# A fused softplus correction, additions moved to the head of a step, three pieces of woven work held back, and an early table load

## The chip, the cores and the metric

The kernel runs on one core of a Trainium2 chip. The time is the device time in microseconds (us) of one execution of the whole kernel; the median of several executions is what two versions are compared by. The core has TensorE (PE: matmuls and transposes, with its weight loads listed as PEld), VectorE (DVE), ScalarE (ACT), GpSimd (POOL) and SyncE (SP), which here only issues DMA transfers. Each engine works through its own instructions in the order in which the program issues them, and waits at an instruction until what it reads or overwrites is free.

## The reference

The input x is 8 images of 256 channels and 96 x 96 points in fp32. Layer 0 normalizes x in groups and adds an attention over channels that works on two-dimensional Fourier transforms. Layer 1, where the change lies, normalizes again and adds a linear attention:

```python
xf = x.reshape(B, C, N)
q = softplus(einsum('dc,bcn->bnd', Wq, xf) + bq)          # d = 32
k = softplus(einsum('dc,bcn->bdn', Wk, xf) + bk)
v = einsum('ec,bcn->ben', Wv, xf) + bv
attn_map = einsum('bdn,ben->bde', k, v)
k_sum = sum(k, axis=-1) + EPS
norm = 1.0 / einsum('bnd,bd->bn', q, k_sum)
out = einsum('bnd,bde,bn->ben', q, attn_map, norm)
x = x + out
```

## The kernel before

An image's activations stay in one of two large SBUF buffers (the "arenas"); the other arena holds what the image needs beside them. The kernel goes through the images one after the other. For each it runs `images` (the rest of layer 0), `layer1`, and `output` (adds layer 1's result and stores it, while layer 0 of the next image begins). The program is written out in the order in which each engine is to work; there is no scheduler that reorders it.

**Woven work.** While image b is in `images`, `layer1` and `output`, the generator `pair_sums(b + 1)` gathers sums of products for the next image. `weave` resumes it as often as the number that the running stage yields; fractions add up. Call each resumption a product: it issues four matmuls (L343) for one third of a group `u` (u = 0 to 11, then a short one for u = 12). In its first third a group also makes the next group's operands, `pair(u + 1)`: for even u + 1 one addition on GpSimd (L391) and one subtraction on VectorE (L392), for odd ones both on GpSimd. In its second third it turns blocks for the group after that, `turn_blocks(u + 2)`: two 32 x 32-block transposes of 128 x 768 on VectorE (L369), ahead of them for even ones two small copies (L364, L365), and after odd ones a DMA that stores both halves of the turned blocks to DRAM (`xtd`, L372) and the load of further input. "Turn 12", the last, is short (L356, L358), and is stored to `xtm` (L359). It writes into the place that the `xtd` transfer after turn 11 reads.

**layer1.** Group statistics on VectorE (L308) and small matmuls (`gm_b`, `gv_b`, `l1b`) give the scaled weights `wkq`. Then come three parts:

- the *kq stage*: for s = 0 to 5 and c = 0 (k) and 1 (q), eight matmuls fill a PSUM tile of 128 x 384 (L812). VectorE stores max(z + bias, 0) in `kq(c, s)` (L814); ScalarE stores exp(-|z + bias|) in `ex` (Abs L816, Exp L817). PSUM tiles of this tag are five in rotation.
- the *kx loop*: softplus is max(z, 0) + log(1 + e). The function `softplus(c, s)` forms u = 1 + e on VectorE (L834), the rounding error (u - 1) - e (L835), lets ScalarE take log(u) (L836) and subtracts the error from z (L837); `close()` later adds the logarithm (L843). Per step s, TensorE transposes k (L867, copied by ScalarE, L868), then three times a piece of x (eight transposes into two PSUM tiles, L878, copied by L881 on ScalarE or L883 on VectorE), and sums k times x in `kx` (L850). The q parts of softplus are worked off in the second half of the loop.
- the *end*: `kx` is copied (`kxs`, L897) and transposed (`kxT`), k's sum gives the denominators (`den`, L917), VectorE forms their reciprocals (`rec`, L921), and at the start of `output` matmuls spread them (L946).

The generator's yields in `layer1` are 2 and 1 in the statistics, 2 ahead of the kx loop, and three times 1 at the end.

Of the kernel before, what the change touches and what calls it, by code (L numbers as in the profile page):

```python
# [73 lines left out]
def two_layer_kernel(ctx: ExitStack, tc: tile.TileContext, x, w1t, b1, w2t, b2, w3, b3, wot, temp,  # L74
                     wqt, bq, wkt, bk, wvt, bv, gavg, gmat, tmat, out):
    nc = tc.nc
    B, C, H, W = x.shape
# [3 lines left out]
    CH = 384  # L81
# [3 lines left out]
    NS = NC // NB  # L85
# [9 lines left out]
    one = ctx.enter_context(tc.tile_pool(name="one", bufs=1))  # L95
    two = ctx.enter_context(tc.tile_pool(name="two", bufs=2))
# [22 lines left out]
    def ps_tile(name):  # L119
        return psum.tile([P, 512], F32, tag="ps", name=name)  # L120
# [57 lines left out]
    for j in range(4):  # L178
        s = slice(32 * j, 32 * j + 32)
# [20 lines left out]
    epsb = const.tile([P, 1], F32, name="epsb")  # L200
# [131 lines left out]
    s0 = {}  # L332
    R2 = 0.5 ** 0.5

    def pair_sums(b):

        acc = [acc_tile(f"acc{c}_{b}") for c in range(2)]
        CB = C + 2
# [37 lines left out]
        def pair(u):  # L376

            eo = ring_tile(f"eo_{b}_{u}").rearrange("p (q c n) -> p q c n", q=NQ, c=2)
            nq, np_ = (NQ, P) if u < NG else (1, W)
            ft, gt = (t[0:np_, 0:nq, u % 2] for t in turned(b))  # L380
            e, o = (eo[0:np_, 0:nq, c, 1:C + 1] for c in range(2))
            nc.gpsimd.memset(eo[0:np_, 0:nq, :, 0:CB:CB - 1], 1.0 if u < NG else R2)  # L382
            if u == 0:
                nc.gpsimd.memset(eo[0:32, 0:nq, :, 0:CB:CB - 1], R2)
            if u in (0, NG):
                w = R2 if u else pw
                nc.vector.tensor_scalar_mul(o, gt, w)
                nc.vector.scalar_tensor_tensor(e, in0=ft, scalar=w, in1=o, op0=ALU.mult, op1=ALU.add)
                nc.vector.scalar_tensor_tensor(o, in0=ft, scalar=w, in1=o, op0=ALU.mult, op1=ALU.subtract)
            else:  # L390
                nc.gpsimd.tensor_add(e, ft, gt)  # L391
# [4 lines left out]
        ahead = pair(0)  # L396
        turn_blocks(1)
        yield
        for u in range(NG + 1):
            eo, nq, np_ = ahead  # L400
            for q in range(nq):
                if q == 0 and u < NG:
                    ahead = pair(u + 1)
                if q == 1 and u + 2 <= NG:
                    turn_blocks(u + 2)
                if (u, q) == (NG - 1, 1):
                    wl = ring_tile(f"wl_{b}")[:, 0:6 * C].rearrange("p (k o) -> p k o", k=KC)
                    for o, v in enumerate((w1t, w2t, w3)):
                        nc.sync.dma_start(out=wl[:, :, o * C:(o + 1) * C], in_=v.rearrange("(k p) o -> p k o", p=P))
                products(eo, q, np_, u == 0 and q == 0, u == NG)  # L410
                yield
# [258 lines left out]
    def images(b):  # L670
# [53 lines left out]
        for i in range(NC):  # L724
            if i % 8 == 0:
                v16 = []
# [33 lines left out]
            if i >= WI:  # L760
                yield 2.5 if i > WI else 1
        for p in pending:
            yield 1
            project(*p)
        st1s[b] = st1

# [2 lines left out]
    def layer1(b):  # L769
# [7 lines left out]
        nc.sync.dma_start(out=wvs, in_=wvt.rearrange("(k p) o -> p k o", p=P))  # L777
        for k in range(KC):
            nc.scalar.activation(wkq[:, k], wkq0[:, k], AF.Copy, scale=rstd[:, k:k + 1])
        pb = ps_tile(f"l1b_{b}")  # L780
        for c in range(2):
            for k in range(KC):
# [9 lines left out]
        def columns_of(s, j):  # L792

            return (s, 2 * NS - 1 - s, 2 * NS + s, NC - 1 - s)[j] * CH
# [3 lines left out]
        def kq(c, s):  # L798


            k, i = ((s // 2, s % 2) if s < 4 else (0, s - 2)) if c == 0 else ((1, s + 2) if s < 4 else (0, s))
            o = LO + NS * CH + i * CH
            return y_of(b)[:, k, o:o + CH]

        for s in range(NS):
            n = slice(s * CH, (s + 1) * CH)
            for c in range(2):
                ps = ps_tile(f"kq_{b}_{s}_{c}")
                for k in range(KC):
                    for j in range(NB):  # L810
                        o = columns_of(s, j)
                        nc.tensor.matmul(ps[32 * j:32 * j + 32, 0:CH], lhsT=wkq[:, k, c],  # L812
                                         rhs=x[:, k, o:o + CH], start=(k == 0), stop=(k == KC - 1))
                nc.vector.tensor_scalar(kq(c, s), ps[:, 0:CH], scalar1=bkqs[:, c:c + 1], scalar2=0.0,  # L814
                                        op0=ALU.add, op1=ALU.max)
                nc.scalar.activation(ex[:, c, n], ps[:, 0:CH], AF.Abs, bias=bkqs[:, c:c + 1])  # L816
                nc.scalar.activation(ex[:, c, n], ex[:, c, n], AF.Exp, scale=-1.0)  # L817
            if s == 1:
                nmb = own[:, 0:C].rearrange("p (k n) -> p k n", k=KC)
                for k in range(KC):  # L820
                    nc.vector.tensor_scalar_mul(nmb[:, k, :], ones, nmean[:, k:k + 1])
                    nc.vector.tensor_scalar_mul(wvs[:, k, :], wvs[:, k, :], rstd[:, k:k + 1])

        zero = own[:, 5 * C:5 * C + 1]
        nc.scalar.activation(zero, ex[:, 1, NS * CH - 1:NS * CH], AF.Copy, scale=0.0)

        late = []

        def softplus(c, s):

            n = slice(s * CH, (s + 1) * CH)
            z, e = kq(c, s), ex[:, c, n]
            u = two.tile([P, CH], F32, tag="v16", name=f"spu_{b}_{c}_{s}")
            nc.vector.tensor_scalar_add(u, e, 1.0)  # L834
            nc.vector.scalar_tensor_tensor(e, in0=u, scalar=1.0, in1=e, op0=ALU.subtract, op1=ALU.subtract)  # L835
            nc.scalar.activation(u, u, AF.Ln, bias=zero)  # L836
            nc.vector.tensor_sub(z, z, e)  # L837
            late.append((z, u))

        def close():  # L840

            for z, u in late:
                nc.vector.tensor_add(z, z, u)  # L843
            late.clear()
# [12 lines left out]
        softplus(0, 0)  # L857
# [4 lines left out]
        close()  # L862
        nc.vector.tensor_add(bvs, bvs, pv[:, 0:C])
        for s in range(NS):
            pk = ps_tile(f"kT_{b}_{s}")
            for i in range(CH // P):
                nc.tensor.transpose(pk[:, i * P:(i + 1) * P], kq(0, s)[:, i * P:(i + 1) * P], ident)  # L867
            nc.scalar.copy(kq(0, s), pk[:, 0:CH])  # L868
            if s + 1 < NS:
                softplus(0, s + 1)  # L870
            for i in range(s * CH // P, (s + 1) * CH // P):
                xt = [slots[2 * (i % 4) + jj] for jj in range(2)]
                for jj in range(2):
                    pt = ps_tile(f"xT_{b}_{i}_{jj}")
                    for j in range(2):
                        o = columns_of(s, 2 * jj + j) + i % (CH // P) * P
                        for k in range(KC):
                            nc.tensor.transpose(pt[:, j * C + k * P:j * C + (k + 1) * P], x[:, k, o:o + P], ident)  # L878
                    src = pt.rearrange("p (j n) -> p j n", j=2)
                    if jj or i % 6 > 1:  # L880
                        nc.scalar.copy(xt[jj][:, :, 0:C], src)  # L881
                    else:
                        nc.vector.tensor_copy(xt[jj][:, :, 0:C], src)  # L883
                close()
                if s >= NS // 2 and i % (CH // P):
                    softplus(1, 2 * s - NS + i % (CH // P) - 1)
                if len(pend) == 3:
                    for p in pend:
                        add_kx(*p)
                    pend = []  # L890
                pend.append((i, xt, kq(0, s)[:, i % (CH // P) * P:(i % (CH // P) + 1) * P]))
        close()
# [195 lines left out]
```

## Time and profile before

| what | value |
|---|---|
| median of 3 runs | 2651.48 us (2646.25 to 2654.46) |
| the profiled execution's own time | 2650.85 us |
| its span | 2649.0 us |
| TensorE busy | 2509.3 us, 95% of the span |
| VectorE busy | 1789.0 us, 68% |
| ScalarE busy | 1155.9 us, 44% |
| GpSimd busy | 865.6 us, 33% |
| one image, from one `images` to the next | 320.9 us (images 1 to 3) |

The span is the time from the first to the last instruction in the profile; the execution's own time has the launch and the end beside it. Busy time is that of instructions that an engine executes; waiting is idle. A line of the timeline gives the start, the duration, the engine, the line of the kernel, what is written and read with its shape, how many instructions were merged, and in brackets how long the engine had been idle and who released it.

### The profile page before, as it was taken

To read this page: it belongs to the slowest core of one execution; us is meant where nothing else is said; L and a number is where in the kernel's file an instruction comes from. 1 tells how busy PE (TensorE), PEld (TensorE's weight loads), DVE (VectorE), ACT (ScalarE), POOL (GpSimd) and SP (SyncE) were. 2 spreads that over 40 slices of the span, in tenths; PEclk is the share of its full clock that TensorE was granted. 3 is DMA by queue.
4 is the path that set the end of the run, shared out by engine and by line. 5 is a ranking of instruction groups with operands and counts; after the bars stand their busy time and mean duration, and the time that the engine had idled before them with its cause. 6 is when DMAs were issued, how large, how long until landed. Compare 5 with 4: busy or idle time off the path is not lost. (4 is left out here: it accounts for less than half of the span.)

```text
span 2649.0 us, 41157 instructions
## 1 busy us (share of the span) xinstructions
PE 2509.3 (95%) x15580; PEld 1730.2 (65%) x15580; DVE 1789.0 (68%) x3449; ACT 1155.9 (44%) x1985; POOL 865.6 (33%) x817
## 2 busy tenths in 40 slices
PE   3799999999999999999999999999999999999987
PEld 3775666757677576766668566685666757667544
DVE  3457866577756777568675686757866678766766
ACT  0035353453634526344353544435354353534554
POOL 2213514136042451324422343223523135141311
PEclk8899999999999999999999999999999999999999
DMA  9872628637195461935629264492636826286003
GB/s 210 238 216 60 166 71 270 205 67 189 40 313 161 106 173 57 315 120 143 153 90 305 80 167 129 159 316 42 166 89 230 245 60 179 58 289 210 1 7 144
DMA packets 282797, 413.27 MB, mean 156 GB/s; under 512 B 40772, under 2 KB 208872, under 8 KB 282600
## 3 DMA queue, kind: packets, MB, share of 16 engines
q1 hardware_dynamic: 274304, 406.16, 53.2%
q10 hardware_dynamic: 8296, 4.49, 0.8%
q8 instruction: 123, 2.02, 0.3%
q14 instruction: 74, 0.61, 0.1%
HBM read 256.72 MB, written 153.86 MB: 155 GB/s over the span
## 5 line engine op out<-in xcount | busy, mean ns | idle before, releaser
L710 PE MATMUL z<-arena,mz 128*128 128x384 f32 (+1 forms) x2304 | 593.4, 491 | 0.0
L718 PE MATMUL po<-e,wo 128*128 128x384 f32 x1536 | 527.6, 487 | 1.7 <-ACT e L755 1.7
L754 POOL TENSOR_TENSOR e<-e 128x768 f32<-128x768 f32 x192 | 348.4, 1815 | 552.7 <-ACT e L753 529.3
L343 PE MATMUL acc<-eo 128*128 128x257 f32 (+2 forms) x2368 | 437.1, 336 | 50.0 <-POOL eo L382 23.0
L343 PEld LDWEIGHTS acc<-eo 128*128 128x128 f32 (+1 forms) x2368 | 383.8, 194 | 143.9 <-issue 42.4
L710 PEld LDWEIGHTS z<-arena,mz 128*128 128x128 f32 (+1 forms) x2304 | 310.5, 164 | 236.0 <-issue 51.9
L718 PEld LDWEIGHTS po<-e,wo 128*128 128x128 f32 x1536 | 290.0, 190 | 204.7 <-ACT e L755 7.2
L749 DVE TENSOR_TENSOR e<-z,xT 128x768 f32<-128x768 f32 x384 | 361.9, 950 | 75.4 <-PE z L710 74.9
L647 PEld LDWEIGHTS y<-tm,arena 96*128 96x128 f32 x3072 | 365.9, 195 | 52.9 <-issue 18.9
L647 PE MATMUL y<-tm,arena 96*128 96x128 f32 x3072 | 385.7, 281 | 15.3 <-DMA arena<-xtd 6.4
L753 ACT ACTIVATE e<-e 128x1536 f32<-128x1536 f32 x192 | 284.5, 1482 | 195.2 <-DVE e L749 193.3
L391 POOL TENSOR_TENSOR eo<-arena 128x768 f32<-128x768 f32 x88 | 184.5, 2096 | 536.3 <-DVE arena L369 473.2
L720 DVE TENSOR_TENSOR arena<-arena,po 128x384 f32<-128x384 f32 x384 | 209.9, 553 | 190.0 <-PE po L718 190.0
L755 ACT ACTIVATE e<-e 128x768 f32<-128x768 f32 x192 | 162.0, 844 | 367.1 <-POOL e L754 363.2
L986 POOL TENSOR_TENSOR arena<-arena,po 128x384 f32<-128x384 f32 x180 | 179.1, 1014 | 224.0 <-ACT po L985 224.0
L369 DVE STREAM_TRANSPOSE arena<-arena 128x768 f32<-128x768 f32 x192 | 175.7, 953 | 32.5 <-DMA xtd<-arena 23.0
L299 DVE BATCH_NORM_STATS2 st<-arena 128x6 f32<-128x384 f32 x384 | 194.4, 548 | 0.0
L654 ACT COPY ys<-y 128x4 f32<-128x4 f32 (+1 forms) x200 | 32.4, 162 | 363.8 <-DVE arena L653 363.7
L878 PE MATMUL xT<-ident,arena 128*128 128x128 f32 x1152 | 148.4, 277 | 10.0 <-ACT xT L881 9.6
L878 PEld LDWEIGHTS xT<-ident,arena 128*128 128x128 f32 x1152 | 127.2, 142 | 32.0 <-issue 13.6
L985 ACT COPY po<-o 128x384 f32<-128x384 f32 x180 | 79.0, 485 | 157.4 <-PE o L977 152.4
L653 DVE COPY arena<-y 128x384 f32<-128x384 f32 (+1 forms) x200 | 109.1, 546 | 40.8 <-PE y L647 38.6
(225 smaller groups left out, 2493.1 us busy)
## 6 DMA issues: line engine op xcount, KB each, us to landing
xtd<-arena SPq DMA_DIRECT2D x48, 1536.0 KB
arena<-xtd SPq DMA_DIRECT2D x192, 384.0 KB
arena<-in_x_dram SPq DMA_DIRECT2D x96, 768.0 KB
out_dram<-arena SPq DMA_DIRECT2D x192, 384.0 KB
arena<-in_x_dram SPq DMA_DIRECT2D x376, 192.0 KB
tm<-rx SPq DMA_DIRECT2D x96, 159.0 KB
wl<-in_w1t_dram SPq DMA_DIRECT2D x8, 256.0 KB
wl<-in_w2t_dram SPq DMA_DIRECT2D x8, 256.0 KB
```

Of the source, the lines that this page charges most:

```text
L299: nc.vector.bn_stats(out=st[:, k, c, :], in_=x_of(b)[:, k, c * CH:(c + 1) * CH])
L343: nc.tensor.matmul(acc[c][:, m * (C + 1):m * (C + 1) + C + 1 - m * P], lhsT=eo[0:np_, q, c, 1 + m * P:1 + (m + 1) * P], rhs=eo[0:np_, q, c ...
L391: nc.gpsimd.tensor_add(e, ft, gt)
L647: nc.tensor.matmul(pu[:, o:o + P], lhsT=xt[:, s, k * P:(k + 1) * P], rhs=tm[:, n:n + P], start=True, stop=True)
L710: nc.tensor.matmul(out[:, 0:CH].rearrange("p (h q) -> p h q", q=PR), lhsT=columns(mz, k, c, j), rhs=yz[:, k, f, :, o:o + PR], start=(k == ...
L718: nc.tensor.matmul(po[:, 0:CH], lhsT=wo[:, k, m * P:(m + 1) * P], rhs=e[:, k, :], start=(k == 0), stop=(k == KC - 1))
L720: nc.vector.tensor_add(x[:, m, n], x[:, m, n], po[:, 0:CH])
L749: nc.vector.tensor_add(e[:, 2 * c:2 * c + 2, :].rearrange("p t (q h) -> p t q h", h=H), pz[:, 0:CH].rearrange("p (h q) -> p q h", h=H).uns ...
L753: nc.scalar.activation(e, e, AF.Square)
L754: nc.gpsimd.tensor_add(e[:, 0:2, :], e[:, 0:2, :], e[:, 2:4, :])
L878: nc.tensor.transpose(pt[:, j * C + k * P:j * C + (k + 1) * P], x[:, k, o:o + P], ident)
L986: nc.gpsimd.tensor_add(x[:, m, r], x[:, m, r], t)
```

## The change

Layer 0's `pair_sums` gets a way to hold three pieces of its work back: turn 10, pair 10 and turn 11. In images with b > 0 they are put into `held` where they were due, and `layer1` of the image before lets them go: turn 10 after step s = 1 of the kq stage, pair 10 in step s = 3 of the kx loop, turn 11 after `kxs`. Turn 12 and pair 11 are not held. The yields change: the last two projections of `images` yield 1.5 each instead of 1, and `layer1` yields 1 more after the weights are scaled. So every product from the 24th on comes earlier in the program.

A first Exp of one column, `warm`, is issued after the weights are scaled. In the kq stage k's rounding error is formed at once (`rest(0, s)`) and enters the eviction, which becomes one instruction max(z + bias, rest); q keeps its eviction. The scaling of `nmb` and `wvs` moves from s = 1 to s = 2. In the kx loop the logarithm is taken in place with a bias of one, `log(c, s)`; the additions of the logarithm, `close(c, s)`, for k stand first in a step; q is worked off one part per step; the order of TensorE's transposes in a step is x, kx of the step before, x, k, x; and VectorE copies two of a step's six x tiles instead of two in every two steps.

```diff
+    held = {}
+    def release(key):
+        held.pop(key, lambda: None)()
     def pair_sums(b):
+        def prepare(key, step):
+            if b and key in (("turn", 10), ("pair", 10), ("turn", 11)):
+                held[key] = step
+            else:
+                step()
...
                 if q == 0 and u < NG:
-                    ahead = pair(u + 1)
+                    prepare(("pair", u + 1), lambda u=u: make(u + 1))
                 if q == 1 and u + 2 <= NG:
-                    turn_blocks(u + 2)
+                    prepare(("turn", u + 2), lambda u=u: turn_blocks(u + 2))
...
         for p in pending:
-            yield 1
+            yield 1.5
             project(*p)
...
             nc.scalar.activation(wkq[:, k], wkq0[:, k], AF.Copy, scale=rstd[:, k:k + 1])
+        warm = one.tile([P, 1], F32, tag="warm", name=f"warm_{b}")
+        nc.scalar.activation(warm, epsb, AF.Exp)
+        yield 1
...
+        def rest(c, s):
+            e = ex[:, c, s * CH:(s + 1) * CH]
+            u = two.tile([P, CH], F32, tag="v16", name=f"spu_{b}_{c}_{s}")
+            nc.vector.tensor_scalar(u, e, scalar1=-1.0, scalar2=-1.0, op0=ALU.mult, op1=ALU.add)
+            nc.vector.scalar_tensor_tensor(u, in0=u, scalar=1.0, in1=e, op0=ALU.add, op1=ALU.add)
+            return u
...
-                nc.vector.tensor_scalar(kq(c, s), ps[:, 0:CH], scalar1=bkqs[:, c:c + 1], scalar2=0.0,
-                                        op0=ALU.add, op1=ALU.max)
+                pss.append(ps[:, 0:CH])
                 nc.scalar.activation(ex[:, c, n], ps[:, 0:CH], AF.Abs, bias=bkqs[:, c:c + 1])
                 nc.scalar.activation(ex[:, c, n], ex[:, c, n], AF.Exp, scale=-1.0)
+            nc.vector.tensor_scalar(kq(1, s), pss[1], scalar1=bkqs[:, 1:2], scalar2=0.0, op0=ALU.add, op1=ALU.max)
+            nc.vector.scalar_tensor_tensor(kq(0, s), in0=pss[0], scalar=bkqs[:, 0:1], in1=rest(0, s), op0=ALU.add, op1=ALU.max)
             if s == 1:
+                release(("turn", 10))
+            if s == 2:
                 nmb = own[:, 0:C].rearrange("p (k n) -> p k n", k=KC)
...
+        def log(c, s):
+            e = ex[:, c, s * CH:(s + 1) * CH]
+            nc.scalar.activation(e, e, AF.Ln, bias=ones[:, 0:1])
+        def close(c, s):
+            nc.vector.tensor_add(kq(c, s), kq(c, s), ex[:, c, s * CH:(s + 1) * CH])
...
+        log(0, 0)
         yield 2
...
         for s in range(NS):
+            close(0, s)
+            last, pend = pend, []
+            turn_x(3 * s)
+            for p in last:
+                add_kx(*p)
+            turn_x(3 * s + 1)
             pk = ps_tile(f"kT_{b}_{s}")
...
             nc.scalar.copy(kq(0, s), pk[:, 0:CH])
+            turn_x(3 * s + 2)
             if s + 1 < NS:
-                softplus(0, s + 1)
...
+                log(0, s + 1)
+            log(1, s)
+            u = rest(1, s)
+            nc.vector.tensor_add(kq(1, s), kq(1, s), u)
+            if s:
+                close(1, s - 1)
+            if s == 3:
+                release(("pair", 10))
+        close(1, NS - 1)
...
         nc.vector.tensor_copy(kxs, kx[:, 0:C + 1])
         yield 1
+        release(("turn", 11))
```

Here `turn_x(i)` is the body of the old loop over pieces: eight transposes of x and two copies, the first copy on VectorE for i % 3 = 0 and 1.

More of the change, by code (lines that the diff above doesn't have):

```diff
@@ L333, in two_layer_kernel, with make @@
     R2 = 0.5 ** 0.5
+    held = {}
+    def release(key):
+        held.pop(key, lambda: None)()
     def pair_sums(b):
+        ready = {}
+        def prepare(key, step):
[3 more added lines that the diff above has]
+                step()
+        def make(u):
+            ready[u] = pair(u)
         acc = [acc_tile(f"acc{c}_{b}") for c in range(2)]
@@ L395, in pair_sums @@
         turn_blocks(0)
-        ahead = pair(0)
+        make(0)
         turn_blocks(1)
@@ L399, in pair_sums @@
         for u in range(NG + 1):
-            eo, nq, np_ = ahead
+            eo, nq, np_ = ready.pop(u)
             for q in range(nq):
                 if q == 0 and u < NG:
-                    ahead = pair(u + 1)
+                    prepare(("pair", u + 1), lambda u=u: make(u + 1))
                 if q == 1 and u + 2 <= NG:
-                    turn_blocks(u + 2)
+                    prepare(("turn", u + 2), lambda u=u: turn_blocks(u + 2))
                 if (u, q) == (NG - 1, 1):
@@ L803, in kq @@
             return y_of(b)[:, k, o:o + CH]
+        def rest(c, s):
[4 more added lines that the diff above has]
+            return u
         for s in range(NS):
             n = slice(s * CH, (s + 1) * CH)
+            pss = []
             for c in range(2):
@@ L822, in layer1 @@
                     nc.vector.tensor_scalar_mul(wvs[:, k, :], wvs[:, k, :], rstd[:, k:k + 1])
[L824 to L844, printed above, removed]
+        def log(c, s):
[3 more added lines that the diff above has]
+            nc.vector.tensor_add(kq(c, s), kq(c, s), ex[:, c, s * CH:(s + 1) * CH])
         kx = acc_tile(f"kx_{b}")
@@ L856, in layer1, with turn_x @@
         pend = []
-        softplus(0, 0)
+        def turn_x(i):
+            s = i // 3
+            xt = [slots[2 * (i % 4) + jj] for jj in range(2)]
+            for jj in range(2):
+                pt = ps_tile(f"xT_{b}_{i}_{jj}")
+                for j in range(2):
+                    o = columns_of(s, 2 * jj + j) + i % 3 * P
+                    for k in range(KC):
+                        nc.tensor.transpose(pt[:, j * C + k * P:j * C + (k + 1) * P], x[:, k, o:o + P], ident)
+                src = pt.rearrange("p (j n) -> p j n", j=2)
+                if jj or i % 3 == 2:
+                    nc.scalar.copy(xt[jj][:, :, 0:C], src)
+                else:
+                    nc.vector.tensor_copy(xt[jj][:, :, 0:C], src)
+            pend.append((i, xt, kq(0, s)[:, i % 3 * P:(i % 3 + 1) * P]))
+        assert CH == 3 * P
+        log(0, 0)
         yield 2
@@ L861, in layer1 @@
             nc.tensor.matmul(pv[:, 0:C], lhsT=nmb[:, k, :], rhs=wvs[:, k, :], start=(k == 0), stop=(k == KC - 1))
-        close()
         nc.vector.tensor_add(bvs, bvs, pv[:, 0:C])
         for s in range(NS):
+            close(0, s)
[4 more added lines that the diff above has]
+            turn_x(3 * s + 1)
             pk = ps_tile(f"kT_{b}_{s}")
-            for i in range(CH // P):
-                nc.tensor.transpose(pk[:, i * P:(i + 1) * P], kq(0, s)[:, i * P:(i + 1) * P], ident)
+            for t in range(3):
+                nc.tensor.transpose(pk[:, t * P:(t + 1) * P], kq(0, s)[:, t * P:(t + 1) * P], ident)
             nc.scalar.copy(kq(0, s), pk[:, 0:CH])
+            turn_x(3 * s + 2)
             if s + 1 < NS:
-                softplus(0, s + 1)
[L871 to L892, printed above, removed]
+                log(0, s + 1)
[7 more added lines that the diff above has]
+        close(1, NS - 1)
         for p in pend:
```

## The prediction

> **What bounds the kernel now.** I read the page first, for the engines' shares.
>
> ```profile
> span 2649.0 us, 41157 instructions
> PE 2509.3 (95%) x15580; PEld 1730.2 (65%) x15580; DVE 1789.0 (68%) x3449; ACT 1155.9 (44%) x1985; POOL 865.6 (33%) x817
> ```
>
> TensorE is the bound, and a change pays only where it removes idle TensorE time or adds some. So I cut one image (b = 2, not the last) into stages with the busy time by window: statistics to the first `kq` matmul; the `kq` matmuls; from there to `kxT`; `kxT` to the first `rec` matmul; the start of the output.
>
> ```profile
> core 0: us, PE busy (x) PEld busy (x) DVE busy (x) ACT busy (x) POOL busy (x), PEclk, DMA share, GB/s
> 986.93:992.17 5.24, 3.90 (x55) 3.30 (x56) 3.42 (x8) 1.05 (x4) 1.95 (x2) 1.00 0.23 93
> 992.17:1007.76 15.59, 15.59 (x212) 6.11 (x201) 7.87 (x16) 12.27 (x22) 1.73 (x3) 1.00 0.34 101
> 1007.76:1046.34 38.58, 35.30 (x339) 26.04 (x335) 31.53 (x62) 27.36 (x54) 2.04 (x2) 1.00 0.01 1
> 1046.34:1052.69 6.35, 6.05 (x43) 4.24 (x42) 5.47 (x7) 0.59 (x2) 3.14 (x2) 1.00 0.38 156
> ```
>
> The third column is TensorE's busy time: 3.3 us idle in 38.58, 1.3 in the first stage, next to none in the `kq` stage. There VectorE is half empty, and the change fills it. The timeline of TensorE names the waits:
>
> ```profile
> 1012.63 0.55 PE L867 MATMUL kT<-ident,arena 128*128 128x128 f32 x3 [1.11 <-DVE arena L843]
> 1016.31 0.66 PE L878 MATMUL xT<-ident,arena 128*128 128x128 f32 x4 [0.94 <-ACT xT L881]
> 1052.69 0.93 PE L946 MATMUL rec<-rec,sel 32*128 32x384 f32 x8 [0.30 <-DVE rec L921]
> ```
>
> Undisturbed, a step of the kx loop takes TensorE 4.54 us (kT at 1021.43, 1025.97 and 1030.51).
>
> **Three waits that matter later.** From the timelines of GpSimd, VectorE, ScalarE and the DMA queue:
>
> ```profile
> 1012.28 1.99 POOL L391 TENSOR_TENSOR eo<-arena 128x768 f32<-128x768 f32 x1 [18.39 <-DVE arena L369]
> 1012.83 1.71 DVE L834 TENSOR_SCALAR spu<-arena 128x384 f32<-128x384 f32 x1
> ...
> 1004.03 0.62 DVE L814 TENSOR_SCALAR arena<-kq,bkqs 128x384 f32<-128x384 f32 x1 [0.67 <-PE kq L812]
> 1004.68 0.58 ACT L816 ACTIVATE arena<-kq,bkqs 128x384 f32<-128x384 f32 x1 [0.15 <-DVE arena L814]
> ...
> 116.78 0.38 SPq L372 DMA_DIRECT2D xtd<-arena  x1
> 122.10 0.77 DVE L358 STREAM_TRANSPOSE arena<-arena 96x256 f32<-96x256 f32 x2 [5.85 <-issue]
> ```
>
> First, an L834 of 0.35 us took 1.71 while GpSimd's L391 ran; and L391 started as soon as the turn was done, not where its pair stands in the program. Second, ScalarE's Abs starts as VectorE's read of the same PSUM tile ends. Third, turn 12 (L358) sat until 5.3 us after the DMA of turn 11 was issued, because it overwrites what that DMA reads.
>
> [...] in the last image, after 3.61 us idle, three kT matmuls took 0.90 against 0.55.
>
> **The change, part by part.** All in an image that is not the last; "product" is one resumption of the woven pair sums, 1.45 us of TensorE.
>
> *Images' tail and statistics.* The 1.5s bring one product more before the last projection, the new yield one more before `l1b`. Turn 9 comes forward, out of the statistics. Its two transposes (1.8 us on VectorE), 7 DMA issues on SP, then fall under 1.45 + 2.6 us of product and projection, where VectorE waits: nothing. The constant bv and wvs loads queue behind those DMAs, but wvs is needed a step later than before: nothing. The wait for `wkq` (0.93) is filled by the new product. The warm exponential and its table load (1.28 us) run where ScalarE idles 2.46 us: nothing on TensorE; before, the load was hidden too. **-0.95.**
>
> *kq stage.* TensorE delivers a group every 1.29 us. VectorE's work per step was 2 x 0.54; it becomes ts 0.54 + rest 0.38 + 0.59 + the fused eviction 0.62 = 2.15 against 2.58. But the order is stiff: the ts waits for Abs of c = 1 (0.65 after the group), so c = 0's PSUM tile comes free 2.8 us after the step's matmuls. With five tiles the group that reuses it would start after 3.6: backlog allowed, 0.75. Count from the first `kq` matmul. Step 1's eviction ends at 8.1; turn 10, let go here, runs to 10.3 (0.2 + 0.2 + 2 x 0.9). Step 2: ts to 10.8, then rest meets GpSimd's L391 for pair 10, which nothing holds (its VectorE half is held, not its GpSimd half), and waits until 12.6; the tile is free at 13.9, wanted at 11.6: stall 2.3. The four nmb and wvs instructions (1.0) and step 3 free the next at 16.9, wanted at 16.5: 0.5. Unknown is how much of the lock falls on rest: without it the stalls are 0.85 and 0.5, with the second rest instruction held too some 3.5. I take **+2.8** (0 to 3.5; no gain, the stage was full). The other queues: GpSimd has nothing due; SP nothing.
>
> *kx loop.* Removed: six subtractions of 0.56 and the two-deep `spu` buffers between VectorE and ScalarE. Six copies move from ScalarE (24 instead of 30) to VectorE. Sums per step are fine: ScalarE 4 x 0.49 + 0.4 + 2 x 0.52 = 3.4, VectorE 3.8, both under 4.54. The order is not. `rest(1, s)` reads the tile that `log(1, s)` has just overwritten, so VectorE waits for ScalarE's last instruction of the step, with close(0, s+1), which kT needs, and the copy that frees a PSUM tile queued behind. The ring: last xT matmuls to visible 0.69, copy 0.49, log 0.52, log 0.64; then on VectorE rest 0.38 + 0.59, addition 0.47, close(1) 0.47, close(0) 0.47, copy 0.68; four matmuls 0.44 until the next step's last four start. Sum **5.84 per step**, over TensorE's 4.54, which is all hidden. The first has no close(1) (5.4), the one after step 3 also the held subtraction of pair 10 (6.7). From the end of kq: two products 2.9, bvs 0.9, two turns of x 1.75, kT 0.35, four xT matmuls 0.44, at 6.35 the last four; 2.3 to the end of log(1, 0): 8.7. Steps: 5.4 + 5.84 + 5.84 + 6.7 + 5.84 less 0.5 (no log(0, 6)) = 29.1. Tail: rest, addition, two closes, kxs 2.9. In all 40.7 to kxT against 38.58. **+2.2** (+1 to +3.5); the last product is hidden in the tail.
>
> *kxT to rec.* Turn 11, let go after kxs, ends 1.75 us after kxT starts; its DMA is issued at 1.8 and lands at 7.1 (5.3 as above). Turn 12 is now resumed ahead of the reciprocal: its L358 waits for that landing, 0.77 to 7.9, with the reciprocal (2.56) behind it on VectorE, for which the selecting matmuls wait: 10.5 against 6.35. TensorE has products, den and am until 6.3, then nothing. **+4.2** (3.5 to 4.5). SP: the 96 KB of turn 12 stands ahead of the fetches, which start no later than before.
>
> *After it.* [...] half speed for some 3 us costs 1.5 at most; I take 0.8. The output has two products fewer; where one lacks, GpSimd's 2 x 1.0 per half step shows beside 0.9 of matmul: 0.5. Together **+1.3** (0 to 3).
>
> *Last image.* No products, no turns. kq unchanged. The first kT comes 0.9 earlier with two turns of x done before, but the loop's ring gives that back: kxs at 2611.4 against 2611.67: **-0.3**.
>
> Sum: 7 x (-0.95 + 2.8 + 2.2 + 4.2 + 1.3) = 7 x 9.55 = 67, less 0.3: the profiled execution's 2650.85 (span 2649.0) becomes 2717.5. The median of the runs, 2651.48, is 0.6 above it: **2718**.
>
> **Rivals.** *The DMA is no wait*: turn 12 finds its DMA landed, or covered. For it, in image 2 L358 ran unhindered at 1057.01; against, there 7.6 us lay between issue and turn, here 1 to 2. 4.2 + 0.8 less per image: 2683. *The ring is covered*: if log(1, s) ends while TensorE still has work, the loop is TensorE's, 4.54 a step. It decides when the ring's sum falls under 4.54, that is, if the 1.3 of waiting is absorbed. For it, the engines' sums (3.4, 3.8) leave room; against, each link is a row of the trace. kxT then comes at 32.4 instead of 40.7, 8.3 less per image, the last one 8.4: 2718 - 58 - 8 = **2652**, not slower. With the landing covered too it would be 2617. *The change doesn't hold what it says*: GpSimd's half of pair 10 runs early, which I count; should the framework keep it until step 3, the lock goes: 2708.
>
> **How the numbers follow.** Forecast 0.80, within its own bounds of 7 x (5.5 to 13): 2690 to 2745; landing covered 0.09; ring covered 0.07, half of it within 0.3% (8 us, about what a measurement of this kernel can tell from no change) and half below; something else 0.04. Range 2683 to 2748. Slower 0.92, same 0.04, faster 0.04.
>
> **What would show it.** Right: L358 idle on VectorE for some 4 us in seven images and the rec matmuls waiting 4 us for the reciprocal; kT to kT in the loop near 5.8 us with VectorE waiting for ScalarE's Ln; `kq` matmuls waiting 2 to 3 us for PSUM tiles in step 4; the l1b wait gone. Wrong: kT to kT at 4.5, or a rec wait below 1 us. A total under 2670 would mean that two of the three steps failed.

## The result and the profile after

The changed kernel takes 2742.03 us (median of 4 runs, 2731.53 to 2744.36); in the same session the kernel before takes 2652.97 (2646.25 to 2667.09). The ratio is 1.0316, with a 95% interval of 1.0279 to 1.0352: 3.2% slower. The profiled execution's own time is 2731.53, its span 2729.7.

The page of the kernel after, span, engines and granted clock:

```profile
span 2729.7 us, 41048 instructions
PE 2541.6 (93%) x15580; PEld 1769.0 (65%) x15580; DVE 1782.7 (65%) x3449; ACT 1140.1 (42%) x1937; POOL 860.6 (32%) x817
PEclk8899997999979999999998999999999999999998
```

TensorE executes the same 15580 matmuls, but its busy time grew by 32 us and its idle time by 48. The mean granted clock of the execution fell from 0.984 to 0.962, and the PEclk row shows dips to 7 and 8 where an image ends. The same row of the kernel before has none behind its first two digits:

```profile
PEclk8899999999999999999999999999999999999999
```

The busy time by window of the kernel after, image 2: statistics; `kq` with two products; from there to `kxT`; `kxT` to the first `rec` matmul; the start of the output.

```profile
core 0: us, PE busy (x) PEld busy (x) DVE busy (x) ACT busy (x) POOL busy (x), PEclk, DMA share, GB/s
1015.10:1020.43 5.33, 4.92 (x62) 4.34 (x63) 1.84 (x6) 1.54 (x5) 1.30 (x3) 1.00 0.76 224
1020.43:1039.91 19.48, 18.70 (x229) 9.03 (x219) 15.33 (x31) 15.69 (x28) 1.89 (x2) 1.00 0.07 22
1039.91:1077.22 37.31, 30.56 (x320) 23.60 (x318) 24.58 (x49) 21.48 (x42) 0.00 (x0) 1.00 0.00 1
1077.22:1087.47 10.25, 6.12 (x42) 4.25 (x42) 5.22 (x9) 0.58 (x2) 3.65 (x3) 0.93 0.52 187
1087.47:1105.88 18.41, 18.41 (x102) 11.78 (x103) 9.42 (x21) 4.29 (x10) 8.21 (x9) 0.85 0.94 282
```

The second and third windows together take 56.79 us where the kernel before took 54.17 (15.59 + 38.58; there the two products were counted in the 38.58). The fourth takes 10.25 instead of 6.35, and TensorE is idle for 4.1 of it. The last runs at a mean clock of 0.85. The timeline of TensorE of the kernel after names the waits:

```profile
1034.31 2.94 PE L840 MATMUL kq<-arena,wkq 128*32 128x384 f32 x32 [0.78 <-DVE arena L846]
1053.62 0.52 PE L909 MATMUL kT<-ident,arena 128*128 128x128 f32 x3 [1.02 <-DVE arena L862]
1059.37 0.52 PE L909 MATMUL kT<-ident,arena 128*128 128x128 f32 x3 [1.02 <-DVE arena L862]
1065.98 0.52 PE L909 MATMUL kT<-ident,arena 128*128 128x128 f32 x3 [1.89 <-DVE arena L862]
1087.47 1.66 PE L976 MATMUL rec<-rec,sel 32*128 32x384 f32 x8 [4.04 <-DVE rec L951]
```

There is one short wait in `kq`, a wait for the closing addition (L862) ahead of kT in each step of the loop but the first, 5.75 us from kT to kT with 6.61 after step 3, and one long wait at the end. The timelines of GpSimd, VectorE and SP of the kernel after show what the waits consist of:

```profile
1030.90 1.84 POOL L407 TENSOR_TENSOR eo<-arena 128x768 f32<-128x768 f32 x1 [14.50 <-DVE arena L385]
1031.17 1.84 DVE L828 TENSOR_SCALAR spu<-arena 128x384 f32<-128x384 f32 x1
...
1050.99 0.36 DVE L828 TENSOR_SCALAR spu<-arena 128x384 f32<-128x384 f32 x1 [2.06 <-ACT arena L858]
...
1078.94 0.37 SPq L388 DMA_DIRECT2D xtd<-arena  x1
1084.21 0.77 DVE L374 STREAM_TRANSPOSE arena<-arena 96x256 f32<-96x256 f32 x2 [4.99 <-DMA xtd<-arena]
1084.90 2.51 DVE L951 RECIPROCAL rec<-den 128x384 f32<-128x384 f32 x1
```

The first pair is the lock of `kq`, which is a name for this slowing alone: L828 took 1.84 us beside GpSimd's addition (L407), 0.35 or 0.36 elsewhere in this image. What lies behind it is not shown. The third line is the ring of the loop: VectorE sits for 2.06 us until ScalarE's logarithm (L858). The last three are turn 12: the DMA is issued at 1078.94, L374 starts 5.27 us later, the reciprocal behind it. The list of waits of the whole kernel after shows the last one seven times (who waited for what: us in total, how often, the longest):

```profile
DVE arena L374 <- DMA xtd<-arena: 35.8, 7, 5.4
```

Something else was not in the working. Image 1 of the kernel after, from the end of its output into the next image's attention, by window:

```profile
core 0: us, PE busy (x) PEld busy (x) DVE busy (x) ACT busy (x) POOL busy (x), PEclk, DMA share, GB/s
771.70:780.00 8.30, 7.37 (x39) 4.72 (x37) 4.82 (x15) 2.78 (x9) 4.00 (x5) 0.73 1.02 371
780.00:790.00 10.00, 9.89 (x45) 8.35 (x45) 3.31 (x12) 3.83 (x10) 3.91 (x4) 0.50 0.59 193
790.00:800.00 10.00, 10.00 (x61) 6.38 (x64) 4.14 (x10) 2.84 (x7) 3.55 (x4) 0.70 0.70 228
```

TensorE is busy for 9.89 of 10 us at a clock of 0.50. A first stretch at half speed (a granted clock of 0.50), of 6.8 us, lies at the long wait itself, in all seven images with products, where TensorE was idle for 4.04 to 4.45 us; this second one begins 22 us after the wait has ended (`rec` at 753.60, the stretch at 775.5) and lasts 20.5 us. It happens in images 0, 1 and 3; their stage from attention to the next image takes 76.3 to 76.6 us, that of the other four 68.7, where one such window of 3.4 us stands in the same place.

### The profile page after: what moved, and what is told of

Read it like the earlier page. It is cut to its first block, busy times and chain, and to the rows that moved or that the text cites. A ratio compares the mean times of both kernels' runs of the same rounds, so it can differ in the third digit from the quotient of the medians.

```text
span 2729.7 us, 41048 instructions
## 1 busy us (share of the span) xinstructions
PE 2541.6 (93%) x15580; PEld 1769.0 (65%) x15580; DVE 1782.7 (65%) x3449; ACT 1140.1 (42%) x1937; POOL 860.6 (32%) x817
## 5 line engine op out<-in xcount | busy, mean ns | idle before, releaser
L359 PE MATMUL acc<-eo 128*128 128x257 f32 (+2 forms) x2368 | 445.0, 341 | 49.8 <-POOL eo L398 23.2
L359 PEld LDWEIGHTS acc<-eo 128*128 128x128 f32 (+1 forms) x2368 | 391.1, 198 | 141.9 <-issue 43.3
L663 PEld LDWEIGHTS y<-tm,arena 96*128 96x128 f32 x3072 | 381.7, 202 | 57.9 <-issue 25.9
L663 PE MATMUL y<-tm,arena 96*128 96x128 f32 x3072 | 403.6, 289 | 12.6 <-DMA arena<-xtd 6.6
L407 POOL TENSOR_TENSOR eo<-arena 128x768 f32<-128x768 f32 x88 | 183.5, 2085 | 556.9 <-DVE ksum L934 324.6
L669 DVE COPY arena<-y 128x384 f32<-128x384 f32 (+1 forms) x200 | 109.2, 546 | 48.1 <-PE y L663 43.6
```

The source lines that it names most:

```text
L359: nc.tensor.matmul(acc[c][:, m * (C + 1):m * (C + 1) + C + 1 - m * P], lhsT=eo[0:np_, q, c, 1 + m * P:1 + (m + 1) * P], rhs=eo[0:np_, q, c ...
L663: nc.tensor.matmul(pu[:, o:o + P], lhsT=xt[:, s, k * P:(k + 1) * P], rhs=tm[:, n:n + P], start=True, stop=True)
```

## The experiments

The theory after the result: the waits that the change adds (the ring, turn 12, the lock) are the whole loss, each worth what it measures. The rival: a wait at the image's end is partly cover for something behind it, and what decides there is TensorE's clock or the output's transfers. Edits are against the kernel after, if not said otherwise. "The output" is the stage from the first `rec` matmul to the attention of the next image. y is the first product of that attention; its copies (L669) overwrite the place from which image b's output is stored (`out_dram`), so they wait for those stores.

### Turn 12 behind the reciprocal

```diff
-            if b and key in (("turn", 10), ("pair", 10), ("turn", 11)):
+            if b and key in (("turn", 10), ("pair", 10), ("turn", 11), ("turn", 12)):
...
             nc.vector.reciprocal(rec, pd[:, 0:CH])
+            release(("turn", 12))
```

> The changed kernel with turn 12 held back too and let go behind the reciprocal, so that nothing on VectorE waits for the store of turn 11 ahead of it. Theory (turn 12 waits for the DMA and the reciprocal with it): kxT to the first rec matmul falls from 10.3 to about 6.4 us in seven images (-27 us), and the half-speed clock behind that wait goes too, some 2.7 us an image (-19): 2731 becomes 2685. If the half-speed stretches later in the output come from this wait as well, another 24 go: 2662. Rival (the two products that the output has lost bring the slow clock): the wait goes, the half-speed stretches of 20 us in the output stay in some images, 2685 or above. Rival (turn 12 costs nothing): no change, 2731 to 2744.

Measured: 2744.1 us (2732.24 to 2751.28), ratio to the kernel before 1.0329 [1.0293, 1.0364]. The wait is gone: `kxT` to `rec` takes 6.5 us instead of 10.3. The kernel is not faster. In the timelines of TensorE, VectorE and SP of this run the time comes back 22 us later:

```profile
748.70 0.93 PE L977 MATMUL rec<-rec,sel 32*128 32x384 f32 x8 [0.33 <-DVE arena L372]
...
769.36 0.56 DVE L669 COPY arena<-y 128x384 f32<-128x384 f32 x1 [3.11 <-DMA out_dram<-arena]
770.17 1.26 PE L1008 MATMUL o<-xT,own 32*128 32x384 f32 x2 [4.14 <-ACT ys L670]
...
757.80 0.61 SPq L425 DMA_DIRECT2D wl<-in_w1t_dram  x1
760.90 13.02 SPq L1021 DMA_DIRECT2D out_dram<-arena  x10
```

The copy of y waits for the stores, in the waits of this run seven times:

```profile
DVE arena L669 <- DMA out_dram<-arena: 22.9, 7, 4.1
```

In the kernel after VectorE's copy of y has no such wait in its list; only ScalarE's has, and a short one:

```profile
ACT arena L669 <- DMA out_dram<-arena: 4.2, 5, 1.0
```

And behind the wait of this run the clock is 0.50 for 17 to 27 us, in all seven images; in all it spends 281 us at half speed, the kernel after 212. So taking the 4 us wait for turn 12 away brings nothing by itself here: with it, the stores were done when y came; without it, TensorE waits for them instead, and the clock falls for longer. The rival holds for this wait.

### The correction ahead of the logarithm

```diff
-            log(1, s)
             u = rest(1, s)
+            log(1, s)
```

> The changed kernel with q's rest formed before its logarithm is taken in place, two lines swapped, so that VectorE's rest no longer waits for ScalarE's last instruction of the step. Theory (the ring rest, log): kT to kT in the loop falls from 5.75 to about 4.6 us, the waits for L862 ahead of kT (0.65, 1.02, 1.02, 1.89, 1.02) and of kxs (1.15) go for the most part, some 6 us an image, 8 images: about 2685. Rival (ScalarE or VectorE is too full in the loop, or PSUM tiles run out): the period stays above 5.3 us and the gain is below 15 us: 2716 or more.

Measured: 2687.66 us (2685.58 to 2690.6), 1.0118 [1.009, 1.0146], 54 less than the kernel after. The stage from the `bvs` matmuls to `kxT`, below "the loop's stage", takes 29.5 us instead of 37.3 (the third window above): 7 x 7.8 = 55, and 7.3 more in the last image. The timeline of TensorE of this run, two steps of the loop and the end:

```profile
1042.47 0.49 PE L909 MATMUL kT<-ident,arena 128*128 128x128 f32 x3
1047.01 0.49 PE L909 MATMUL kT<-ident,arena 128*128 128x128 f32 x3
...
1070.03 0.93 PE L976 MATMUL rec<-rec,sel 32*128 32x384 f32 x8 [3.77 <-DVE rec L951]
```

A step takes 4.54 us and nothing in the loop waits; the ring is what made it 5.75. For the loop the theory holds. That 55 and 54 agree so well is luck: 62 us are gained in the loop, and some is given back elsewhere, as the half-speed time rises from 212 to 258 us. One swapped pair of lines is worth more than half of the regression. The swap is not only one of time: `log(1, s)` writes log(1 + e) over e in `ex`, so in the kernel after `rest(1, s)` forms q's correction from the logarithm, where the formula wants e. With the lines swapped it reads e. The instructions are the same in number and shape.

### Both

> Both edits, turn 12 behind the reciprocal and q's rest before its logarithm. If the two waits are separate and all that matters, the gains add: 2731 less 46 to 70 less 46 to 50, so 2612 to 2640, faster than the kernel before (2651). If the waits hide one another or the slow clock comes from the fewer products in the output, above 2645.

Measured: 2666.38 us (2652.89 to 2675.84, 20 runs), 1.0049 [1.0035, 1.0063]. That is 26 to 54 above what was expected: with the ring gone, moving turn 12 does bring 21 us (2687.66 to 2666.38), but not the 4 x 7 of the wait. The copy of y again waits for the stores, 19.8 us in seven images, and the half-speed stretches stand in six.

### Useless matmuls in the wait for `rec`

Behind `am`, six matmuls of 128 x 384 that nothing needs, 3.9 us per image:

```diff
+        if b + 1 < B:
+            pf = ps_tile(f"fill_{b}")
+            for i in range(6):
+                nc.tensor.matmul(pf[:, 0:CH], lhsT=ident, rhs=x[:, 0, i * CH:(i + 1) * CH], start=(i == 0), stop=(i == 5))
+            fill = one.tile([P, 1], F32, tag="fill", name=f"fl_{b}")
+            nc.scalar.copy(fill, pf[:, 0:1])
```

> The changed kernel with six matmuls of 128x384 on data at hand, 3.9 us of TensorE, put behind the am matmuls, where TensorE waits for the reciprocal; a column of their sum is copied into a scratch tile. It adds work and takes no wait away: it separates the wait from the slow clock that follows it. Theory [...]: kxT to rec stays at 10.3 us, but the rec matmuls take 0.93 instead of 1.66 and the products behind them 1.58 instead of 2.94, -2.7 us an image: 2712, and 2690 if the later half-speed stretches have the same cause. Rival (the clock is lowered by something else, as by the sparse matmuls of the output): the clock behind rec stays at half and the time is 2731 or more.

Measured: 2705.18 us (2696.89 to 2714.42), 1.0187 [1.0153, 1.0221]: 37 us faster than the kernel after, with more work in it. The time spent at half speed falls from 212 to 154 us in the profiled executions (2731.53 and 2714.42 us). The 6.8 us at the wait itself are gone in all seven images; a later stretch of 17 to 20 us is left in three. So the half speed at this wait of some 4 us carries a part of the loss (58 us less at a clock of 0.50 are worth 29 at most), and the later stretches have another cause.

### Either half of the change alone

The softplus part alone (nothing held, the projections' yields back at 1, the new yield gone):

```diff
-            if b and key in (("turn", 10), ("pair", 10), ("turn", 11)):
+            if b and key in ():
...
-            yield 1.5
+            yield 1
...
         nc.scalar.activation(warm, epsb, AF.Exp)
-        yield 1
```

> The softplus part alone: the changed kernel with nothing held back and the yields of the kernel before, so that every product and turn comes where it came before. Theory (the parts are separate): no wait of turn 12, kxT to rec 6.4 us; the kq stage has no turn and no stall; the loop keeps its ring, 5.75 us a step, so that the stretch from bvs to kxT is 36.5 to 38 us against 35.8 before: 2650 to 2668, near the kernel before. No further half-speed stretches than before. Rival (most of the loss lies in the softplus part): above 2690.

Measured: 2665.9 us (2662.44 to 2680.43, 12 runs), 1.004 [1.0024, 1.0056]. The loop's stage is 38.6 to 39.7 us against 35.8 before (1010.50, where `bvs` begins, to 1046.34); `kxT` to `rec` is 6.4, as before.

The weaving part alone is the kernel before with `held`, `prepare`, the releases and the new yields, and its own softplus (the scaling of `nmb` and `wvs` moves to s = 2 here too):

> The other part alone: the kernel before with its own softplus, and the changed yields and held pieces (turn 10 let go in the kq stage, pair 10 in step 3, turn 11 after kxs). Theory: kxT to rec 10.3 us, half speed behind it, and longer half-speed stretches in the output as in the changed kernel; no kq stall, since VectorE has room there: 2700 to 2718. Rival (the products that come earlier do no harm, and only softplus does): 2660 or less.

Measured: 2724.7 us (2717.82 to 2729.51), 1.0254 [1.0221, 1.0288], above the range given. The loop's stage is as before (35.6), `kxT` to `rec` 10.3 to 12.4, and the stage from the attention to the next image varies between 68.7 and 76.3, as in the kernel after. Against the kernel before, measured beside them at 2657.12, the softplus part costs 9 us and the weaving 68. The weaving carries most of the regression, and more than its one wait of 4 us per image.

### The weights' load later

On top of "both":

```diff
-                if (u, q) == (NG - 1, 1):
+                if u == NG:
```

> Both edits (turn 12 behind the reciprocal, q's rest first), and the load of the three weight matrices issued one group later, behind instead of ahead of the output's second pair of stores on SP. Theory (with two products fewer TensorE reaches the first y step before the first output stores have landed, and 0.77 MB of weights stand in front of them): the waits of VectorE's copy of y for out_dram (19.8 us in seven images) fall to 10 or less, and with fewer half-speed stretches the time falls from 2666 to 2640 to 2655. Rival (the wait is for stores that the weights do not delay): no change, 2660 to 2672.

Measured: 2637.3 us (2623.18 to 2651.72, 11 runs), 0.992 [0.9896, 0.9944], 29 less. `wl` hangs on a product, so it moved ahead of most stores when the products moved. Of the first twelve stores of an output, SP issued six ahead of it in the kernel before; in the run with turn 12 behind the reciprocal (757.80 in the timeline above) two ahead and ten behind; in this run six again. The waits of "both" for the stores:

```profile
DVE arena L669 <- DMA out_dram<-arena: 19.8, 7, 3.4
```

and the waits of this run for them:

```profile
DVE arena L669 <- DMA out_dram<-arena: 5.8, 6, 2.0
```

The two profiled executions (2669.09 and 2651.72 us) are 17 us apart, and this wait is 14 of it.

### The softplus part with the swap

The softplus part alone and `rest(1, s)` ahead of `log(1, s)`, so no block is held and no product moved:

> The softplus part alone with q's rest formed before its logarithm. Theory (the gain of the loop is real once no product is taken from the output): bvs to kxT about 30 us instead of 35.8, in all eight images, nothing given back in the output: 2600 to 2612, faster than both kernels. Rival (what is gained in the loop is given back in the output, where y waits for the stores of the image before): above 2635.

Measured: 2608.27 us (2606.48 to 2609.64), 0.9817 [0.9789, 0.9846]. **This beats both kernels, by 1.8% and by 4.9%.** Page and timeline of TensorE of this run:

```profile
PEclk8899999999999999999999999999999999999997
```

```profile
1000.93 0.52 PE L908 MATMUL kT<-ident,arena 128*128 128x128 f32 x3 [2.06 <-DVE arena L861]
...
1010.03 0.49 PE L908 MATMUL kT<-ident,arena 128*128 128x128 f32 x3
1014.57 0.49 PE L908 MATMUL kT<-ident,arena 128*128 128x128 f32 x3
```

The loop's stage takes 31.8 us against 35.8 before. The steps are 4.54 in both where nothing disturbs them; before, the second half of the loop had waits that are gone here, as in these two lines of the kernel before's timeline of TensorE:

```profile
1035.13 0.66 PE L878 MATMUL xT<-ident,arena 128*128 128x128 f32 x4 [0.36 <-ACT xT L881]
...
1043.72 1.11 PE L850 MATMUL kx<-xT,arena 128*32 128x257 f32 x8 [0.36 <-ACT xT L881]
```

Idle time is the smaller part of it: 3.28 us in this stage before, 2.06 here. The same 318 matmuls are counted as busy for 32.6 us before and 29.7 here; around a wait they take longer, as the eight of the last line, 1.11 us instead of 0.62.

29 us in seven images, and 8.1 in the last (38.8 to 30.7), of the 43.8 between the spans (2649.0 and 2605.2) come from there. Another 8 are in the images and the attention, where the kernel before shows more single stretches of 3.41 us at half speed (seven against two up to the last image).

Two variants of it. Without `warm`:

> The fastest version so far (softplus part alone with q's rest first, 2608 us) without the early table load. Theory: the load of 1.28 us lay hidden before too, five PSUM tiles let TensorE go on, so the time stays at 2604 to 2612. Rival (the load delays the first fused evictions, which need exp of k): TensorE waits for PSUM in step 1 or 2, up to 1 us an image, 2612 to 2620.

Measured: 2610.52 us (2607.32 to 2610.81), 0.9831 [0.9798, 0.9864]: the early table load is worth nothing that can be measured. With one product moved out of the output (the new `yield 1` put back):

> The same fastest version with the one new yield behind the scaled weights, so that one product moves from the output into the wait for wkq (0.93 us). If a product is worth the wait that it fills: -0.9 us an image, 2602. Theory now (the output needs its products, since the first y step waits there for the stores of the image before[...]): the gain is given back, the stretch from kxT on grows by 1 us or more in some images, 2605 to 2635.

Measured: 2621.71 us (2618.48 to 2628.94), 0.9879 [0.9844, 0.9914]: 13 us are lost for one product moved per image. Its half-speed stretches of 17 to 20 us are in three images (of the profiled execution, 2628.94 us), in the run without this move in none.

### Useless matmuls in the output

On "the weights' load later", in half steps 3 and 4 of the output two matmuls each, 2.6 us per image:

```diff
+                    if 3 <= 2 * s + m < 5:
+                        pf = ps_tile(f"fill_{b}_{s}_{m}")
+                        for i in range(2):
+                            nc.tensor.matmul(pf[:, 0:CH], lhsT=ident, rhs=wo.rearrange("p k c -> p (k c)")[:, 0:CH], start=(i == 0), stop=(i == 1))
+                        fill = one.tile([P, 1], F32, tag="fill", name=f"fl_{b}_{s}_{m}")
+                        nc.scalar.copy(fill, pf[:, 0:1])
```

> Both edits with the weights loaded later (2637 us), with two matmuls of 128x384 on data at hand added in each of two half steps of the output where products are missing (2.6 us of TensorE an image, work that nothing needs). Theory (idle TensorE in the output brings the half-speed stretches of 20 us that follow): with the gap filled they go in most images, some 8 us each, 2637 becomes 2590 to 2625 although work is added. Rival (the slow clock comes from the sparse 32-row matmuls or elsewhere): 2637 or more, by up to 18 us of added work.

Measured: 2618.49 us (2607.07 to 2625.72), 0.9859 [0.982, 0.9899]: 19 us faster for 18 us of useless work. In the profiled execution, which took 2607.07 us and so lies below the median, no half-speed stretch over 3.41 us is left between the start and the last image. So work is what the output lacks once products have been taken from it, even work that nothing needs. The matmuls added are of 128 rows; no run filled the gap with others. Whether only the clock, or the stores too, gained by the delay is not told apart either; VectorE's copy of y no longer waits for them in this run.

### Turn 10 in the first step of the loop

On "the softplus part with the swap", turn 10 alone held:

```diff
-            if b and key in ():
+            if b and key in (("turn", 10),):
...
-            if s == 1:
-                release(("turn", 10))
...
-            if s == 3:
-                release(("pair", 10))
+            if s == 0:
+                release(("turn", 10))
```

> The kernel with k's correction in its own eviction and rest(1, s) ahead of log(1, s), in which turn 10 alone is held back and let go in step 0 of the loop over four steps (2608.27 us without that). There the first kT waits 2.06 us for the closing addition of step 0, which stands behind turn 10 (2.2 us on VectorE) and took 2.13 us beside GpSimd's addition instead of 0.56. Theory: VectorE has idle time later in step 0, so the first kT comes 2 us earlier, seven times: 14 us less, about 2594 us (2588 to 2602). Rival: turn 10 and GpSimd's addition only move on, into the additions of step 1, and the wait turns up in front of the second kT: less than 5 us, 2603 us or more.

The reason for it, in the timelines of VectorE and GpSimd of "the softplus part with the swap": the closing addition stood behind turn 10, beside GpSimd's addition.

```profile
996.58 1.84 DVE L385 STREAM_TRANSPOSE arena<-arena 128x768 f32<-128x768 f32 x2
...
998.57 1.81 POOL L407 TENSOR_TENSOR eo<-arena 128x768 f32<-128x768 f32 x1 [19.07 <-DVE arena L385]
998.65 2.13 DVE L861 TENSOR_TENSOR arena<-arena 128x384 f32<-128x384 f32 x1
```

Measured: 2634.12 us (2615.29 to 2653.41, 12 runs), 0.9918 [0.989, 0.9946]: 26 slower. Locally it did what the theory says. The timeline of TensorE has no wait left:

```profile
1008.20 1.03 PE L895 MATMUL bvs<-wvs,own 128*128 128x256 f32 x4
1010.82 0.49 PE L906 MATMUL kT<-ident,arena 128*128 128x128 f32 x3
1015.56 0.52 PE L906 MATMUL kT<-ident,arena 128*128 128x128 f32 x3
```

The loop's stage takes 29.8 us instead of 31.8. Both theories put the outcome in the loop, and both are wrong. The windows of the output and of the 13.66 us after it, first of this run:

```profile
core 0: us, PE busy (x) PEld busy (x) DVE busy (x) ACT busy (x) POOL busy (x), PEclk, DMA share, GB/s
1048.93:1066.73 17.80, 16.82 (x105) 10.91 (x105) 10.70 (x27) 6.12 (x15) 11.39 (x13) 1.00 1.07 327
1066.73:1080.39 13.66, 13.55 (x64) 10.86 (x63) 4.36 (x15) 4.64 (x11) 4.87 (x6) 0.50 0.83 291
```

then of "the softplus part with the swap":

```profile
1038.84:1056.60 17.76, 16.80 (x104) 10.91 (x104) 10.68 (x27) 6.12 (x15) 11.33 (x13) 1.00 1.03 308
1056.60:1070.26 13.66, 13.35 (x112) 9.80 (x111) 6.65 (x21) 6.80 (x18) 7.23 (x8) 1.00 1.06 379
```

The output takes the same time with the same busy share in both (16.8 of 17.8 us), and no wait of TensorE in it reaches 0.5 us. Then one runs at half speed for 13.65 us and executes 64 matmuls, the other at full speed executes 112. This happens in six of seven images, and costs more than the 14 us gained. What differs is when the output begins, which the last section takes up.

## Why the prediction was right, and where its sum was wrong

The total is within the range, 24 us above the predicted time (2718 against 2742), and the waits named are in the trace. The spans differ by 80.7 us where the sum said 67. Term by term, from the stages of the seven images with products:

| step | predicted, per image | measured, per image |
|---|---|---|
| tail and statistics | -0.95 | -1.7 |
| kq stage and kx loop | +2.8 and +2.2 | +1.2 and +1.5 |
| kxT to rec | +4.2 | +4.0 |
| after it | +1.3 | +6.1 |
| last image, once | -0.3 | +2.9 |

"Measured" is the stage's difference less 1.45 us for each product moved into it, plus that for each moved out.

**Turn 12** was read rightly, from two lines of the kernel before: 4.99 us of waiting on VectorE, 4.04 on TensorE. But the first experiment shows that its 28 us were not a loss that could be taken away alone. **The ring** was worked out as 5.84 us per step and measures 5.75; the wait for the logarithm is where it was put. That it is the cause is shown by the swapped lines.

**The kq stage** was sized too high. The lock came where the step put it (L828 took 1.84 us beside L407), but TensorE waited once, for 0.78 us, not for 2.8. The tile of k in step 2 came free 13.8 us after the first `kq` matmul, as counted (13.9). The count had it wanted by the tenth group of matmuls; in the trace the tenth starts at 1032.04, 2.2 us before that tile is free, and the eleventh waits for it. So the tile that the tenth took was another, and the count was one group too strict. Of the range of 0 to 3.5 the upper half was taken, and the lower was true.

**"After it" failed most**, 1.3 against 6.1, 34 us in seven images. The step counted one half-speed stretch of 3 us behind the wait, at 0.8 us, and 0.5 us for the two missing products. The first was the author's estimate. In the last image of the kernel before, after TensorE was idle for 3.61 us, the clock was 0.50 for 3.41 us; in the kernel after it was 0.50 for 6.8 us at the wait. The runs showed two more things. First, the output's products are not work that can stand anywhere: without them the clock falls to a half again later, for 20.5 us in three images of the kernel after and for 3.4 in four; with one product moved it does so in three images, and with useless matmuls in the gap hardly. Whether idle time or the matmuls of 32 rows that are left bring it is open: in the last full window of 3.41 us ahead of it (from one point of the grid in the last section to the next) TensorE was busy for 67 to 73%, for 16 to 31% with other matmuls than these. In all, this kernel spends 212 us at half speed, the one before 87. Half of the difference, 62 us, is the most that it can cost; the waits and this overlap. Second, the stores to `out_dram` must land before y may be copied, and `wl` is issued with a product, ahead of them. As long as turn 12's wait is there, it hides that.

**The rivals.** "The landing covered", at 2683, ought to be what the first experiment makes. It came to 2744: taking the wait away gave nothing, because it was itself the cover for the stores. "The ring covered", at 2652, is the kernel with the swapped lines; it came to 2688, since that rival had removed 8.3 us per image where 7.8 were there, and the undersized last term remained. The term for the last image missed by 3 us, in its sign too; 2.0 of it lie between `kxT` and `rec`, where the clock is at half speed after and not before, and nothing tells why.

Two errors offset each other in part: kq and the loop 2.3 too high per image, "after it" 4.8 too low. The small slips in the sums (0.54 + 0.38 + 0.59 + 0.62 is 2.13, not 2.15; 40.7 less 38.58 is 2.1, not 2.2) don't matter beside that. The forecast was right in its direction and in the waits that it named, and nearly right in its total by some luck.

## What to carry to other kernels

Before woven work is moved out of a stage that is thin in matmuls, look at what the stage hides (stores that must land before a buffer is written again, loads issued with the woven work) and at the PEclk row of a trial: here one product moved per image, into a wait of 0.93 us, cost 13 us in all. Where two engines work in place on one tile, put the reader of the old value ahead of the writer; here two swapped lines were worth 54 us, and the old value was also the one that the formula wants. A local gain counts only when the whole has been timed: two of these experiments removed a wait exactly as meant and made the kernel no faster.

## What the runs showed of the hardware

**The half-speed stretches lie on a grid.** In each of the fourteen profiled executions, all stretches at a clock of 0.5 begin at whole multiples of 3.413 us from each other and last whole multiples of it (1 to 8, but for the one that the end cuts off). A window below is the 3.413 us from one such grid point to the next. In the run with turn 10 in the loop, for example, the long stretches begin at 428.44, 745.88, 1066.73, 1384.17, 2015.64 and 2336.49 us, that is 93, 94, 93, 185 and 94 times 3.4133 us apart, and last 13.65 us (four times 3.413) or, once, 17.07 (five times). An idle TensorE is not all that comes ahead of half speed: in this run, TensorE was busy for 84% of the last full window before the clock fell, though for only 32% of it with matmuls other than the output's of 32 rows. Nor do these shares decide: image 4 has the same two in that window and keeps its clock.

**Where an output begins on that grid goes with whether the clock falls.** The kernel before, the softplus part alone, the same with the swap, that without `warm`, and the run with turn 10 in the loop issue the same matmuls in the output. From the clock record and the first `o` matmul of their 35 images with products (1048.93 in the window of the run with turn 10 above), the time since the last grid point is:

| time since the last grid point, us | images | half speed in the seventh window |
|---|---|---|
| 0.43 to 2.05 | 25 | 0 |
| 2.19 to 2.94 | 10 | 10 |

In the run with turn 10 in the loop, the images last 317.5, 320.7, 317.5, 320.1, 311.5 and 320.7 us from one output to the next, most of them close to 93 or 94 times 3.413 (317.4 and 320.9), so the unfavourable position came back in six of seven. In the kernel before it is images 0 to 3, one window each, and in three of them another one 65 us later; from one output to the next these images take 320.9 us three times and 319.3 us, the next two 317.7 and 317.6. In the three others no image is hit in that window. This is a regularity of 35 cases and not an experiment: no run shifted the output alone.

Other outputs have other limits. With one product moved, three images at 0.87 to 0.98 are hit for long and four at 1.06 to 1.64 are not; with useless matmuls in the wait for `rec`, three at 1.54 to 2.82 are hit and four at 0.27 to 0.70 are not. In the three runs with turn 12 behind the reciprocal and no matmuls added, all 21 images are hit, wherever they begin (0.08 to 3.13). With the useless matmuls in the output, where it begins at 0.37 to 2.11, one of seven is hit, for one window. So a shift of the output on the grid does not explain what these matmuls gained. Open is why a stretch lasts one window in one kernel and four or five in another.

**The lock was seen on an addition of two tiles too**: in "the softplus part with the swap" L861 took 2.13 us beside a GpSimd addition (L407) instead of 0.56, longer than the TENSOR_SCALAR of the kernel after (L828, 1.84 instead of 0.36).
